# A 3x3 convolution by transformed rows: a fourth row of six with four products for its columns, the last product group added onto a preset bank, and the rows' transform back one row later

## The chip, the core and the metric

The kernel runs on one core of a Trainium2 chip. The metric is the device time of one execution in microseconds. A core has a matrix engine (TensorE, PE in the profile), a vector engine (VectorE, DVE), a scalar engine (ScalarE, ACT), GpSimd (POOL) and SyncE (SP), which issues DMAs. Each engine runs its own instructions in order and waits for others by semaphores. TensorE's results land in PSUM[...].

## The reference

Two layers on an image batch of 4 x 1024 x 56 x 56, all in 32-bit floats. Layer 0 is a bottleneck with a deformable 3x3 convolution; layer 1 is a bottleneck with batch normalisation over the whole batch. The change concerns layer 1's 3x3 convolution, 256 channels to 256, and the preparation of its filters.

```python
# layer 0
r = relu(conv1x1(x, w1, b1))                      # 1024 -> 256
r = relu(deform_conv3x3(r, w2, b2, w_off, b_off)) # offsets by a 3x3 conv, bilinear gather
x = relu(x + conv1x1(r, w3, b3))                  # 256 -> 1024
# layer 1
out = relu(bn(conv(x, w1, b1, 1, 0), g1, be1))    # 1024 -> 256
out = relu(bn(conv(out, w2, b2, 1, 1), g2, be2))  # 3x3, 256 -> 256
out = bn(conv(out, w3, b3, 1, 0), g3, be3)        # 256 -> 1024
return relu(x + softplus(residual_scale)[0] * out)
```

## The kernel before

Layer 0 fills the span to about 2060 us, with layer 1's first 1x1 convolution fused to its end; that one's output y1 goes to DRAM. Near the end of layer 0, while the last image is worked on, a generator `filters` (L651 to 706) prepares layer 1's 3x3 filters in small steps on VectorE. A step is taken by `next(extra, None)` at three of the nine taps of a block (L794).

The 3x3 convolution works on parts: half an image each, eight parts, `parts = [(n, half) ...]`. Rows go through a transform that makes six transformed rows p out of each six input rows (for four output rows, a quad; there are seven quads in a part, so a row p of a part is 128 partitions x 2 channel blocks x 7 x width). Each transformed row needs a one-dimensional convolution of three taps along its columns, with that row's own transformed filter `u[p]` (three taps u0, u1, u2 of 256 x 256). The rows are taken in the order `SEQ = (1, 2, 3, 4, 0, 5)`. Columns are kept as even and odd ones.

A row whose columns are convolved with five products (not in WIN) makes, for an even and an odd output column, products of 196 columns (and one of 203) for each of 2 x 2 blocks of channels: 20 products per row and part. A row in WIN is convolved with four products, 16 per row and part, from sums of taps (`us[p]`) and sums and differences of columns (`vs[p]`, and `v[p]` changed in place). Before, WIN is (2, 4, 5), so a part has 3 x 20 + 3 x 16 = 108 products.

A row p of part i goes through three stages on TensorE, and the loop at L1124 to 1145 interleaves them: the `begin` of a row, then the `end` of the row before it, then the row's own `middle`.

- `begin` (L993): for WIN, us x vs into bank q, then ScalarE writes the odd output columns as -2 q (L998). Otherwise two products into q and one into b; ScalarE copies q to odd (L1011) and -b to even (L1012), and VectorE adds b onto odd (L1015).
- `middle` (L1018), WIN alone: u1 x vs is added onto q, and ScalarE copies q to even (L1022).
- `end` (L1024): for WIN, u2 x v is added onto q, and u0 x v goes into a bank b; VectorE adds q onto odd (L1033) and subtracts b from even (L1034). Otherwise two more products are added onto q, and VectorE subtracts q from even (L1041). Then `end` also does the rows' transform back (L1042 to 1069): after p = 2 a sum and a difference (2 operations), after p = 4 eight operations, after p = 0 and p = 5 one each. The first and the last part also take statistics there (`bn_stats`).

ScalarE may write to the output rows of the next row only once the transform back has read them, since outputs y2 are worked on in place: `TARGET = (0, 0, 1, 2, 3, 3)` names the output row that row p uses as its place, so rows 0 and 1 share one, and rows 4 and 5.

After `end` of rows 2, 4, 0 and 5 the loop computes the next part's `inputs` for the rows that are done (L910 to 952): row transforms, then for WIN rows the column sums, L947 and its neighbour (392 elements each) and an in-place difference (L950, 784), otherwise one operation of 406 elements (L952). `load` (L876) brings the next part's input rows by DMA, and ScalarE normalises them with four activations (L901). `passes` (L1087) lets ScalarE take a middle part's statistics as sums in eight activations (L1095), two after each row, into a small tile `moved`. `reference` and `gather` (L1082, L1104) bring these sums together.

The filter taps of row 0 are written to DRAM (`u0_d`, L688) and read back at the start of the convolution (L854), as the memory is needed in between; those of row 5 are read from the input (L856). `us` of rows 2 and 4 (EARLY) are made in `filters`; those of 1, 3, 0 and 5 in the loop at L1115 to 1123, between the inputs of the first part. `first_rows` (L709) is where the first part's rows are read to, by SyncE, during layer 0.

Of the kernel before, what the change touches and what calls it, by code (L numbers as in the profile page):

```python
# [8 lines left out]
F32 = mybir.dt.float32  # L9
# [19 lines left out]
PIECE = QUADS * W  # L29
SEQ = (1, 2, 3, 4, 0, 5)  # L30
TARGET = (0, 0, 1, 2, 3, 3)
WIN = (2, 4, 5)
EARLY = (2, 4)

SIZES = (512, 512, 512, 512, 384, 384, 320)
STARTS = [sum(SIZES[:j]) for j in range(NJ)]
# [24 lines left out]
def deform_bottleneck_then_bn_bottleneck(  # L61
# [23 lines left out]

    x1_d = dram.tile([N, CIN, HW], F32, tag="x1_d", name="x1_d")
    x1_v = x1_d.rearrange("n (k p) q -> n p k q", p=128)
    u0_d = dram.tile([128, KB * 3 * CB], F32, tag="u0_d", name="u0_d")
    y1_d = dram.tile([N, CB, HW], F32, tag="y1_d", name="y1_d")
    y1_v = y1_d.rearrange("n (k p) q -> n p k q", p=128)  # L90

# [77 lines left out]
    with ExitStack() as l0:  # L169
# [481 lines left out]
        def filters():  # L651


            pool = l1.enter_context(tc.tile_pool(name="filters", bufs=1, side="right"))
            many = KB * (HALF + 2) * W
            ends = pool.tile([128, many], F32, tag="rows", name="ends")
            each = KB * 3 * CB
            w_0, w_2 = ends[:, :each], ends[:, each : 2 * each]
            for p in range(1, 5):
                u[p] = pool.tile([128, KB, 3, CB], F32, tag=f"u{p}", name=f"u{p}")  # L660
            u1, u2, u3, u4 = (u[p].rearrange("p h j o -> p (h j o)") for p in range(1, 5))
            rows = b_w2.rearrange("(h p) (i j) o -> i p h j o", p=128, j=3)
# [24 lines left out]
            nc.vector.tensor_scalar_mul(w_0, w_0, 0.25)  # L687
            nc.sync.dma_start(u0_d, w_0)  # L688
            yield
            flat = pool.tile([128, many], F32, tag="rows", name="rows")  # L690
            first_rows.append(flat.rearrange("p (h r w) -> p h r w", h=KB, w=W))
            raw_rows(first_rows[0][:, :, : HALF + 1], 0, 0)
            yield
            for p in EARLY:
                us[p] = pool.tile([128, KB, CB], F32, tag=f"us{p}", name=f"us{p}")
                yield from column_filters(p)

        def column_filters(p):

            w_0, w_1, w_2 = (u[p][:, :, j] for j in range(3))  # L700
            nc.vector.tensor_add(us[p], w_0, w_2)
            yield
            nc.vector.tensor_add(w_1, w_1, us[p])
            nc.vector.tensor_scalar_mul(w_1, w_1, 0.5)
            yield
            nc.vector.tensor_sub(us[p], us[p], w_1)
            yield

        def raw_rows(to, n, half):  # L709
# [70 lines left out]
        for i, (n, j, k) in enumerate(taps):  # L780
# [10 lines left out]
            if (n, j, k) == (N - 1, 1, 0):  # L791
                l0a.close()
                extra = filters()
            if extra and k in (1, 4, 7):  # L794
                next(extra, None)
            budget += share * SIZES[j]
            passed = (STARTS[j] + SIZES[j] * k / TAPS) / HW
# [38 lines left out]
    with l1:  # L836
# [9 lines left out]
        for p in range(6):  # L846
# [10 lines left out]
        for p in range(6):  # L857
            if p not in us:
                us[p] = wino.tile([128, KB, CB], F32, tag=f"us{p}", name=f"us{p}")
# [98 lines left out]

        half_w = W // 2

        def rows_of(n, half, r):
# [14 lines left out]
        def products(ps, terms, first=False, last=False, alone=False):  # L978

            for o in range(KB):  # L980
                of = slice(o * 128, (o + 1) * 128)
                pairs = [(wt[:, h, of], x[:, :, h]) for h in range(KB) for wt, x in terms]
                for j, (wt, x) in enumerate(pairs):
                    nc.tensor.matmul(  # L984
                        ps[:, o].rearrange("p r c -> p (r c)"),
                        wt,
                        x,
                        start=first and j == 0 and (alone or o == 0),
                        stop=last and j == len(pairs) - 1,
                        skip_group_check=not alone,  # L990
                    )

        def begin(i, p):  # L993
            even, odd = halves(i, p)
# [9 lines left out]
                first=True,  # L1004
            )
            b = bank(psb, "b", i, p, half_w + 1)
            products(b, [(u[p][:, :, 1], x0)], first=True, last=True, alone=True)
# [7 lines left out]
            nc.vector.tensor_add(odd, odd, b[..., 1:])  # L1015
            return q

        def middle(i, p, q):  # L1018
            if p in WIN:
                even, _ = halves(i, p)  # L1020
                products(q, [(u[p][:, :, 1], vs[p][..., :half_w])])
                nc.scalar.copy(even, q)  # L1022

        def end(i, p, q):  # L1024

            n, half = parts[i]
            even, odd = halves(i, p)
            if p in WIN:
                x0, x1 = v[p][..., :half_w], v[p][..., PW // 2 : PW // 2 + half_w]
                products(q, [(u[p][:, :, 2], x1)], last=True)  # L1030
                b = bank(psb, "b", i, p, half_w)
                products(b, [(u[p][:, :, 0], x0)], first=True, last=True, alone=True)
                nc.vector.tensor_add(odd, odd, q)  # L1033
                nc.vector.tensor_sub(even, even, b)  # L1034
            else:
                products(
                    q,
                    [(us[p], vs[p][..., :half_w]), (u[p][:, :, 2], vs[p][..., 1 : 1 + half_w])],
                    last=True,
                )  # L1040
                nc.vector.tensor_sub(even, even, q)  # L1041
            r = [rows_of(n, half, k) for k in range(4)]  # L1042

            def stats(k):
# [70 lines left out]
        ds = {0: load(0)}  # L1115
        for ps in ((1, 2), (3, 4), (0,), (5,)):
            inputs(0, ds[0], ps)
            for p in ps:
                if p not in WIN:
                    nc.vector.tensor_add(us[p], u[p][:, :, 0], u[p][:, :, 1])  # L1120
                elif p not in EARLY:
                    for _ in column_filters(p):
                        pass
        before, passing = None, iter(())  # L1124
        for i, p in [(i, p) for i in range(len(parts)) for p in SEQ] + [(len(parts), None)]:
            begun = begin(i, p) if p is not None else None
            if before is not None:
                j, q, _ = before
                end(*before)
                if j + 1 < len(parts) and q in (2, 4, 0, 5):  # L1130
                    inputs(j + 1, ds[j + 1], (q - 1, q) if q in (2, 4) else (q,))
                if q == SEQ[-1]:
                    if j == 0:
                        reference()
                    elif j not in ENDS:
# [9 lines left out]
            before = (i, p, begun)  # L1145
# [243 lines left out]
```

## Time and profile before

| | us |
|---|---|
| median of 3 runs | 2878.97 |
| lowest and highest | 2876.26, 2881.56 |
| the profiled execution, its own time | 2866.03 |
| its span on the core | 2864.2 |
| the 3x3 convolution of layer 1 in it | about 2097 to 2411 |
| idle time of PE at the start of that convolution (to 2105.23) | 8.43 |

TensorE's granted clock was 0.99 of full speed over the span. A 32-bit product is listed as two records, and records overlap: their listed length (329 to 339 ns at 196 columns) is longer than the distance from one to the next. In the lines of groups, the columns are: line, engine, operation, output and inputs, shape and count; then busy time and the mean of one in ns; then idle time just before, with what ended it. In the timeline: start, length, engine, line, operation, count, and in brackets the idle time before it. In the lines of waits: the engine with its line, what it waited for, the total, how many times, the longest.

### The profile page before, as it was taken

Reading aid. Unit: us, or ns where it says so; the run is one execution under the profiler, and the core shown is the slowest. Engines: PE = TensorE matmul, PEld = TensorE weight load, DVE = VectorE, ACT = ScalarE, POOL = GpSimd, SP = SyncE. Lnnn points to the kernel's source line nnn. Section 1 sums busy time; section 2 is a strip of 40 time slices with the busy share of each in tenths; the row PEclk is TensorE's granted clock in tenths of the full one; section 3 lists DMA queues with packets and bytes.
Section 4 is the critical chain, followed back from the end, with each engine's and each line's share of the span. In section 5 each row is a group of like instructions: output and inputs, shape, how many; then the busy total and the mean of one; then the engine's idle time right before and its main releaser. Section 6 shows DMA issues by size and latency. Waiting matters only on the chain.

```text
span 2864.2 us, 39301 instructions
## 1 busy us (share of the span) xinstructions
PE 2775.4 (97%) x12001; PEld 1924.8 (67%) x12001; DVE 2070.1 (72%) x4961; ACT 1503.3 (52%) x3069; POOL 1120.8 (39%) x998
## 2 busy tenths in 40 slices
PE   9978999999999999999999989999989998999999
PEld 4445566677666666667666657667779998955554
DVE  2187788888787789787888897877679886344444
ACT  2145555665556556556555656666644454244444
POOL 0065555466566556556555575544400000000000
PEclk9999999999999999999999999999999998999999
DMA  7699998999989989999998999999621102059997
GB/s 249 190 358 317 325 344 316 340 336 327 379 293 374 348 289 346 329 340 350 341 351 268 372 322 350 346 336 334 220 100 48 47 23 80 1 192 309 308 303 262
DMA packets 337109, 792.17 MB, mean 277 GB/s; under 512 B 33240, under 2 KB 183296, under 8 KB 336896
## 3 DMA queue, kind: packets, MB, share of 16 engines
q0 software_dynamic: 127296, 462.48, 45.0%
q1 hardware_dynamic: 179120, 275.78, 28.8%
q10 hardware_dynamic: 30480, 51.39, 4.7%
q8 instruction: 95, 1.56, 0.2%
q14 instruction: 118, 0.97, 0.1%
HBM read 640.68 MB, written 143.48 MB: 274 GB/s over the span
## 4 chain that ended last, share of the span: by engine, by line
PE 84%; DMA 7%; DVE 5%; ACT 2%; issue 2%; SPq 0%; POOL 0%; ACTq 0%; DVEq 0%; POOLq 0%
PE acc L540 19%; PE pf L1157 11%; PE pr L596 11%; PE acc L622 11%; PE acc L312 10%; PE q L984 7%; PE stp L512 6%; DMA g<-table,idxs 5%; DVE s L487 3%; PE acc_g L1207 2%; PE b L984 2%; PE pm L361 2%; PE ftp L391 1%; PE tp L1188 1%; PE pa L1157 1%
## 5 line engine op out<-in xcount | busy, mean ns | idle before, releaser
L475 POOL DMA_INDIRECT g<-table,idxs x900 | 1110.3, 1234 | 939.5 <-DVE s L487 283.5
L487 DVE SCALAR_TENSOR_TENSOR s<-g,wts,s 128x256 f32<-128x256 f32 (+1 forms) x2700 | 1173.3, 476 | 310.6 <-ACT s L485 299.9
L540 PE MATMUL acc<-sts,w 128*128 128x256 f32 (+2 forms) x3528 | 723.5, 355 | 5.3 <-ACT sts L518 4.1
L540 PEld LDWEIGHTS acc<-sts,w 128*128 128x128 f32 x3528 | 601.2, 190 | 56.3 <-ACT sts L518 7.4
L485 ACT ACTIVATE s<-g,wts 128x256 f32<-128x256 f32 x900 | 427.0, 511 | 285.7 <-DMA g<-table,idxs 149.4
L596 PE MATMUL pr<-r,w 128*128 128x512 f32 (+2 forms) x896 | 367.7, 548 | 19.6 <-ACT pr L592 12.8
L312 PE MATMUL acc<-xt,w 128*128 128x448 f32 x896 | 356.7, 544 | 10.7 <-DMA xt<-in_x_dram 10.7
L622 PE MATMUL acc<-x1t,c1w 128*128 128x512 f32 (+2 forms) x896 | 359.0, 542 | 6.0 <-ACT acc L618 3.8
L1157 PE MATMUL pf<-y,c3w 128*128 128x448 f32 x844 | 317.4, 539 | 0.0
L512 PEld LDWEIGHTS stp<-ident,s 128*128 128x128 f32 (+1 forms) x1800 | 212.7, 142 | 137.6 <-issue 83.4
L596 PEld LDWEIGHTS pr<-r,w 128*128 128x128 f32 x896 | 165.0, 192 | 160.6 <-issue 84.3
L1321 DVE SCALAR_TENSOR_TENSOR x1f<-pf,sc_bn,x1f 128x448 f32<-128x448 f32 x211 | 144.2, 683 | 172.5 <-PE pf L1157 159.3
L312 PEld LDWEIGHTS acc<-xt,w 128*128 128x128 f32 x896 | 168.6, 192 | 148.8 <-issue 140.6
L512 PE MATMUL stp<-ident,s 128*128 128x128 f32 (+1 forms) x1800 | 252.2, 274 | 16.6 <-DVE s L487 11.5
L1157 PEld LDWEIGHTS pf<-y,c3w 128*128 128x128 f32 x844 | 160.4, 190 | 156.8 <-issue 118.4
L622 PEld LDWEIGHTS acc<-x1t,c1w 128*128 128x128 f32 x896 | 168.0, 191 | 144.9 <-issue 90.5
L518 ACT COPY sts<-stp 128x512 f32<-128x512 f32 (+2 forms) x504 | 242.0, 529 | 13.1 <-PE stp L512 12.8
L1329 ACT ACTIVATE x1f<-x1f,sh_bn 128x448 f32<-128x448 f32 x224 | 148.3, 667 | 173.7 <-DVE x1f L1321 172.0
L607 ACT ACTIVATE x1t<-pr,ch 128x512 f32<-128x512 f32 (+2 forms) x224 | 141.6, 632 | 124.3 <-PE pr L596 121.9
L632 ACT COPY y<-acc 128x512 f32<-128x512 f32 (+2 forms) x112 | 59.3, 529 | 195.7 <-PE acc L622 195.7
L522 DVE TENSOR_TENSOR sts<-sts 128x512 f32<-128x512 f32 (+2 forms) x252 | 155.1, 615 | 0.6
L592 ACT COPY pr<-xr 128x512 f32<-128x512 f32 (+2 forms) x224 | 121.4, 542 | 4.7 <-DMA xr<-in_x_dram 0.4
(221 smaller groups left out, 2391.3 us busy)
## 6 DMA issues: line engine op xcount, KB each, us to landing
xt<-in_x_dram SPq DMA_DIRECT2D x112, 448.0 KB
x1f<-x_d SPq DMA_DIRECT2D x112, 448.0 KB
out_dram<-x1f ACTq DMA_DIRECT2D x111, 448.0 KB
xr<-in_x_dram SPq DMA_DIRECT2D x128, 256.0 KB
x_d<-x1t SPq DMA_DIRECT2D x128, 256.0 KB
table<-ft SPq DMA_DIRECT2D x56, 384.0 KB
g<-table,idxs POOLq DMA_INDIRECT x900, 7.3
xr<-in_x_dram SPq DMA_DIRECT2D x64, 192.0 KB
```

Source lines behind the costliest of these rows:

```text
L312: nc.tensor.matmul(acc, w1[:, k, h * 128 : (h + 1) * 128], xts[n, j, k - k % 2][:, k % 2, :], start=start, stop=(k == KC - 1), skip_group_ ...
L475: nc.gpsimd.indirect_dma_start(out=g[:m], out_offset=None, in_=tables[n].rearrange("r q c -> r (q c)"), in_offset=bass.IndirectOffsetOnAxi ...
L485: nc.scalar.activation(s[:m], g[:m, 0:CB], AF.Copy, scale=wt[:, 0])
L487: nc.vector.scalar_tensor_tensor(s[:m], g[:m, corner * CB : (corner + 1) * CB], wt[:, corner], s[:m], ALU.mult, ALU.add,)
L512: nc.tensor.transpose(banks[h][:, t * 128 : t * 128 + m], s[:m, h * 128 : (h + 1) * 128], ident[:m, :m],)
L518: nc.scalar.copy(to, banks[h][:, :size].rearrange("p (e q) -> p e q", e=2))
L522: nc.vector.tensor_sub(sts[:, 5:7, :half], sts[:, 1:4:2, :half], sts[:, 0:2, :half])
L540: nc.tensor.matmul(sums[i], w2[:, a, k], sts[:, b, :half], start=(k == 0 and i % 2 == 0), stop=(k == TAPS - 1), skip_group_check=True,)
L596: nc.tensor.matmul(z, w3[:, h, k * 128 : (k + 1) * 128], r2[:, h, :size], start=False, stop=(h == KB - 1), skip_group_check=True,)
L622: nc.tensor.matmul(z, c1w[:, k, h * 128 : (h + 1) * 128], x1ts[k], start=False, stop=(i == KC // 2 - 1), skip_group_check=True,)
L984: nc.tensor.matmul(ps[:, o].rearrange("p r c -> p (r c)"), wt, x, start=first and j == 0 and (alone or o == 0), stop=last and j == len(pai ...
L1157: nc.tensor.matmul(pz, c3w[:, h, k * 128 : (k + 1) * 128], y2[n][:, h, j * BLK : (j + 1) * BLK], start=(h == 0), stop=(h == KB - 1),)
```

## The change

Row 3 joins WIN and EARLY: its columns are convolved with four products as well, and its `us` is made in the early filters. Those steps are now taken at every odd tap (four of nine). Both outer rows' taps (0 and 5), with their `us` sums made in the early filters, are written to DRAM and read back, in place of row 0's taps alone; the buffer of the sums carries the tag "us2", which us[2] uses after them. At the convolution's start one addition is left (us of row 1).

In the convolution itself, from row 0 of the first part on (`on_top`), ScalarE puts -q into a bank b after a WIN row's middle, the four products u0 x v of the row's end are added onto it without a start flag, and ScalarE writes -b to the even columns, in place of VectorE's subtraction. The products into b before that no longer start for each block of output channels, but once for the bank.

The rows' transform back becomes a function of its own, `back`, and is done one row later, ahead of the begin of the row after next; `reference`, the passes' start and `gather` move along. `moved` is put into the tile of y1's statistics.

```diff
-WIN = (2, 4, 5)
-EARLY = (2, 4)
+WIN = (2, 3, 4, 5)
+EARLY = (2, 3, 4)
...
-    u0_d = dram.tile([128, KB * 3 * CB], F32, tag="u0_d", name="u0_d")
+    outer_d = dram.tile([2, 128, KB * 4 * CB], F32, tag="outer_d", name="outer_d")
...
             nc.vector.tensor_scalar_mul(w_0, w_0, 0.25)
-            nc.sync.dma_start(u0_d, w_0)
             yield
+            for i, w in enumerate((w_0, w_2)):
+                other = pool.tile([128, KB, CB], F32, tag="us2", name=f"other_{i}")
+                w = w.rearrange("p (h j o) -> p h j o", h=KB, j=3)
+                if i == 0:
+                    nc.vector.tensor_add(other, w[:, :, 0], w[:, :, 1])
+                else:
+                    yield from column_filters(w, other)
+                to = outer_d[i].rearrange("p (j o) -> p j o", j=4 * KB)
+                nc.sync.dma_start(to[:, : 3 * KB], w.rearrange("p h j o -> p (h j) o"))
+                nc.sync.dma_start(to[:, 3 * KB :], other)
...
-            if extra and k in (1, 4, 7):
+            if extra and k % 2:
                 next(extra, None)
...
-        u[0] = wino.tile([128, KB, 3, CB], F32, tag="u0", name="u0")
-        nc.sync.dma_start(u[0], u0_d.rearrange("p (h j o) -> p h j o", h=KB, j=3))
-        u[5] = wino.tile([128, KB, 3, CB], F32, tag="u5", name="u5")
-        nc.sync.dma_start(u[5], b_w2.rearrange("(h p) (i j) o -> i p h j o", p=128, j=3)[2])
...
+        for p, i in ((0, 0), (5, 1)):
+            u[p] = wino.tile([128, KB, 3, CB], F32, tag=f"u{p}", name=f"u{p}")
+            us[p] = wino.tile([128, KB, CB], F32, tag=f"us{p}", name=f"us{p}")
+            of = outer_d[i].rearrange("p (j o) -> p j o", j=4 * KB)
+            nc.sync.dma_start(u[p].rearrange("p h j o -> p (h j) o"), of[:, : 3 * KB])
+            nc.sync.dma_start(us[p], of[:, 3 * KB :])
+        us[1] = wino.tile([128, KB, CB], F32, tag="us1", name="us1")
+        nc.vector.tensor_add(us[1], u[1][:, :, 0], u[1][:, :, 1])
...
-                        start=first and j == 0 and (alone or o == 0),
+                        start=first and j == 0 and o == 0,
...
+        def on_top(i, p):
+            return (i, SEQ.index(p)) >= (0, 4)
...
         def middle(i, p, q):
             if p in WIN:
                 even, _ = halves(i, p)
                 products(q, [(u[p][:, :, 1], vs[p][..., :half_w])])
-                nc.scalar.copy(even, q)
+                if on_top(i, p):
+                    ends[i, p] = bank(psb, "b", i, p, half_w)
+                    nc.scalar.mul(ends[i, p], q, -1.0)
+                else:
+                    nc.scalar.copy(even, q)
...
-                b = bank(psb, "b", i, p, half_w)
-                products(b, [(u[p][:, :, 0], x0)], first=True, last=True, alone=True)
+                b = ends.pop((i, p), None)
+                top = b is not None
+                if not top:
+                    b = bank(psb, "b", i, p, half_w)
+                products(b, [(u[p][:, :, 0], x0)], first=not top, last=True)
                 nc.vector.tensor_add(odd, odd, q)
-                nc.vector.tensor_sub(even, even, b)
+                if top:
+                    nc.scalar.mul(even, b, -1.0)
+                else:
+                    nc.vector.tensor_sub(even, even, b)
...
-        moved = wino.tile([128, 2, KB, between * CUTS], F32, tag="moved", name="moved")
+        moved = y1_stats.rearrange("p h s -> p (h s)")[:, : 2 * KB * between * CUTS].rearrange(
+            "p (f h c) -> p f h c", f=2, h=KB
+        )
...
-        before, passing = None, iter(())
-        for i, p in [(i, p) for i in range(len(parts)) for p in SEQ] + [(len(parts), None)]:
+        before, behind, passing = None, None, iter(())
+        for i, p in [(i, p) for i in range(len(parts)) for p in SEQ] + [(len(parts), None)] * 2:
+            if behind is not None:
+                back(*behind)
+                if behind[1] == SEQ[-1]:
+                    if behind[0] == 0:
+                        reference()
+                    elif behind[0] not in ENDS:
+                        passing = passes(behind[0])
+                if behind == (len(parts) - 1, SEQ[-2]):
+                    gather()
             begun = begin(i, p) if p is not None else None
+            behind = None
             if before is not None:
                 j, q, _ = before
                 end(*before)
+                behind = j, q
                 if j + 1 < len(parts) and q in (2, 4, 0, 5):
                     inputs(j + 1, ds[j + 1], (q - 1, q) if q in (2, 4) else (q,))
-                if q == SEQ[-1]:
-                    if j == 0:
-                        reference()
-                    elif j not in ENDS:
-                        passing = passes(j)
-                for _ in range(2):
-                    next(passing, None)
-                if (j, q) == (len(parts) - 1, SEQ[-2]):
-                    gather()
+            for _ in range(2):
+                next(passing, None)
```

More of the change, by code (lines that the diff above doesn't have):

```diff
@@ L695, in filters, with column_filters @@
                 us[p] = pool.tile([128, KB, CB], F32, tag=f"us{p}", name=f"us{p}")
[L696 to L701, printed above, removed]
+                yield from column_filters(u[p], us[p])
+        def column_filters(w, other):
+            w_0, w_1, w_2 = (w[:, :, j] for j in range(3))
+            nc.vector.tensor_add(other, w_0, w_2)
             yield
-            nc.vector.tensor_add(w_1, w_1, us[p])
+            nc.vector.tensor_add(w_1, w_1, other)
             nc.vector.tensor_scalar_mul(w_1, w_1, 0.5)
-            yield
-            nc.vector.tensor_sub(us[p], us[p], w_1)
+            nc.vector.tensor_sub(other, other, w_1)
             yield
@@ L852, in deform_bottleneck_then_bn_bottleneck @@
             vs.append(wino.tile([128, QUADS, KB, width], F32, tag=f"vs{p}", name=f"vs{p}"))
-        u[0] = wino.tile([128, KB, 3, CB], F32, tag="u0", name="u0")
-        nc.sync.dma_start(u[0], u0_d.rearrange("p (h j o) -> p h j o", h=KB, j=3))
-        u[5] = wino.tile([128, KB, 3, CB], F32, tag="u5", name="u5")
-        nc.sync.dma_start(u[5], b_w2.rearrange("(h p) (i j) o -> i p h j o", p=128, j=3)[2])
-        for p in range(6):
-            if p not in us:
-                us[p] = wino.tile([128, KB, CB], F32, tag=f"us{p}", name=f"us{p}")
+        for p, i in ((0, 0), (5, 1)):
[6 more added lines that the diff above has]
+        nc.vector.tensor_add(us[1], u[1][:, :, 0], u[1][:, :, 1])
         sum_t = wino.tile([128, KB, QUADS, W], F32, tag="sum_t", name="sum_t")
@@ L976, in bank, with products @@
             return t[:, : KB * QUADS * width].rearrange("p (o r c) -> p o r c", o=KB, c=width)
-        def products(ps, terms, first=False, last=False, alone=False):
+        def products(ps, terms, first=False, last=False):
             for o in range(KB):
@@ L987, in products @@
                         x,
-                        start=first and j == 0 and (alone or o == 0),
+                        start=first and j == 0 and o == 0,
                         stop=last and j == len(pairs) - 1,
-                        skip_group_check=not alone,
+                        skip_group_check=True,
                     )
+        def on_top(i, p):
+            return (i, SEQ.index(p)) >= (0, 4)
         def begin(i, p):
@@ L1006, in begin @@
             b = bank(psb, "b", i, p, half_w + 1)
-            products(b, [(u[p][:, :, 1], x0)], first=True, last=True, alone=True)
+            products(b, [(u[p][:, :, 1], x0)], first=True, last=True)
             for o in [slice(o, o + 1) for o in range(KB)] if p == 1 else [slice(0, KB)]:
@@ L1016, in begin @@
             return q
+        ends = {}
         def middle(i, p, q):
@@ L1021, in middle @@
                 products(q, [(u[p][:, :, 1], vs[p][..., :half_w])])
-                nc.scalar.copy(even, q)
+                if on_top(i, p):
[3 more added lines that the diff above has]
+                    nc.scalar.copy(even, q)
         def end(i, p, q):
-            n, half = parts[i]
             even, odd = halves(i, p)
@@ L1041, in end, with back @@
                 nc.vector.tensor_sub(even, even, q)
+        def back(i, p):
+            n, half = parts[i]
             r = [rows_of(n, half, k) for k in range(4)]
@@ L1117, in deform_bottleneck_then_bn_bottleneck @@
             inputs(0, ds[0], ps)
[L1118 to L1123, printed above, removed]
-        before, passing = None, iter(())
-        for i, p in [(i, p) for i in range(len(parts)) for p in SEQ] + [(len(parts), None)]:
+        before, behind, passing = None, None, iter(())
[9 more added lines that the diff above has]
+                    gather()
             begun = begin(i, p) if p is not None else None
+            behind = None
             if before is not None:
@@ L1144, in deform_bottleneck_then_bn_bottleneck @@
                 ds[i + 1] = load(i + 1)
-            before = (i, p, begun)
+            before = (i, p, begun) if p is not None else None
     sc2, sh2 = scale_shift(y2_stats, KB, cols("g2", KB), cols("be2", KB), "bn2")
```

## The prediction

> **What bounds the kernel now.** I read the page's sums and its chain first, then stretches of one part each (a part is half an image, eight parts in all) through the 3x3 convolution of the second layer at 2097 to 2411 us, then the waits, and last the order of instructions at the places where an engine stands.
>
> ```profile
> PE 2775.4 (97%) x12001; PEld 1924.8 (67%) x12001; DVE 2070.1 (72%) x4961; ACT 1503.3 (52%) x3069; POOL 1120.8 (39%) x998
> PE 84%; DMA 7%; DVE 5%; ACT 2%; issue 2%; SPq 0%; POOL 0%; ACTq 0%; DVEq 0%; POOLq 0%
> ...
> 2143.00:2180.00 37.00, 37.00 (x220) 36.76 (x219) 36.92 (x61) 11.11 (x19) 0.56 (x4) 1.00 0.14 45
> 2180.00:2217.00 37.00, 36.98 (x219) 36.41 (x218) 34.88 (x52) 19.29 (x39) 0.75 (x5) 1.00 0.15 48
> 2217.00:2254.00 37.00, 36.85 (x214) 35.59 (x213) 32.11 (x49) 19.26 (x38) 0.37 (x3) 1.00 0.15 46
> ```
>
> The first two lines say that TensorE carries the end. The last three are stretches of 37 us (start:end, length, PE, PEld, DVE, ACT, POOL, clock, DMA share, GB/s): TensorE is full in all of them, but VectorE is too in the second part (36.92 of 37) and has only 5 us to spare later, while ScalarE has 18. So work taken off TensorE pays only where VectorE keeps up. TensorE's busy time is flattered by overlapping records. The first product of consecutive parts starts (L1011's releaser) 37.15 us apart on average, and 108 products of 0.337 us (two records of 0.168) make 36.4, so 0.75 us per part is standing time. The waits show whom it stands for:
>
> ```profile
> PEld q L984 <- ACT y L1022: 3.7, 12, 0.6
> PEld q L984 <- ACT y L998: 1.7, 6, 0.4
> ```
>
> A four-product row ("WIN") hands its bank q to ScalarE twice and then adds to it. TensorE needs other products to fill that time. Without them the gap looks like the stage's end:
>
> ```profile
> 2400.14 1.50 PE L984 MATMUL b<-v,u 128*128 128x196 f32 x8
> 2404.35 2.98 PE L984 MATMUL q<-vs,u 128*128 128x196 f32 x8 [2.71 <-ACT y L998]
> 2407.93 2.98 PE L984 MATMUL q<-v,u 128*128 128x196 f32 x8 [0.59 <-ACT y L1022]
> ```
>
> From the end of a group to the next on the same bank takes 0.6 to 0.76 us ([...]ScalarE's 0.52, signals), and eight records after the pause cost 2.98 instead of 1.36.
>
> **The skill.** "TensorE: Matmul & The Clock Gate", Part 1: after an idle window the array runs at half rate until it has been busy a window long. The trace agrees on the half rate (2.98 against 1.36), though a pause of 2.71 us sufficed here. "PSUM — Partial Sum Buffer", the four PSUM rules: writes of ScalarE leave the accumulate bits as they are, and a matmul without start adds where a bit is set. So the preset bank can work; layer 0 of this kernel shows the same pattern (L592 into pr, then L596). "Perfetto Trace Analysis", on the most contended engine: weight-load time tells more than matmul busy; here it does (35.59 of 37 where PE reads 36.85).
>
> **The change, part by part.**
>
> *Row 3 with four products.* Per part 20 products (16 of 196 columns, 4 of 203) become 16: 4 x 0.336 plus the 203-column surcharge of 4 x 0.008 is 1.38 us. Eight parts: **-11.1**.
>
> *VectorE per part.* Row 3's inputs gain two operations of 392 elements and an in-place one of 784 and lose one of 406. By start-to-start pace (0.475, 0.885, 0.49): 2 x 0.475 + 0.885 - 0.49 = +1.35.
>
> ```profile
> L950 DVE TENSOR_TENSOR v<-v 128x784 f32<-128x784 f32 x21 | 20.3, 965 | 0.5
> L952 DVE SCALAR_TENSOR_TENSOR vs<-v 128x406 f32<-128x406 f32 x21 | 12.0, 572 | 0.0
> L1034 DVE TENSOR_TENSOR y<-y,b 128x392 f32<-128x392 f32 x24 | 13.4, 559 | 5.5 <-ACT y L1022 2.9 <-PE b L984 2.3
> L1022 ACT COPY y<-q 128x392 f32<-128x392 f32 x24 | 12.4, 518 | 33.8 <-PE q L984 33.7
> ```
>
> The ends lose the subtraction of L1034 in rows 2, 4 and 5 and row 3's end goes from two operations to one: -4 x 0.475 = -1.9. Net -0.55 per part from part 1 on; VectorE drops to about 31.6 of a 35.8 us part. ScalarE takes four writes of 0.52 more, +2.1 per part, for 21 of 36. Neither is the bound by its sum, but ScalarE's order now matters: its write stands between two product groups.
>
> *Stage start.* Before, VectorE adds us for rows 1 and 3 (1.29 us together) ahead of the first inputs; after, only row 1's: TensorE starts 0.6 us earlier, **-0.6**. Off VectorE's list in the head also go us0's addition (0.6) and u5's four filter operations (2.2). But row 3's extra halves (about 2) and part 1's inputs of rows 3 and 4 (4.5) now all stand ahead of the transform back of row 4, because that comes a row later. Row 5's first product is read (L998) only once that transform has written its target: at 2146.28 before, by my list at about 2149 after. Row 5's middle waits, and its cover is spent: **+2.8**, and +0.5 in part 1, where VectorE is still full. Bounds: nothing, if VectorE gains on its list, to +4.5.
>
> *New waits between groups.* Row 3's begin is followed by the end of row 2 and then row 3's middle. Where row 2's end was held, q3's begin and middle meet, and the round trip of 0.76 is open. I find that in parts 2, 3, 4, 5, 7: **+3.8** (0 to 5.3). ScalarE's new preset is queued, in order, behind the statistics passes and the four rows of the next part:
>
> ```profile
> 2227.34 0.83 ACT passed L1095
> 2228.17 0.03 issue
> 2228.20 0.19 ACT passed L1095
> 2228.39 1.05 ACT rows L901
> 2229.43 0.93 ACT passed L1095 x2
> 2230.36 3.04 ACT rows L901 x3
> 2233.40 0.93 ACT passed L1095 x2
> 2234.34 0.40 ACT y L1022
> ```
>
> This is before's chain of waits: about 7 us of ScalarE ahead of a copy that TensorE needs. In part 2 row 3's end comes out 1.1 us late behind it (**+1.1**). In part 6 row 2's middle waits for L998's successor, queued behind passes and rows, while TensorE has only the last rows of part 5 to fill: 3.1 to 3.5, taken 3.3, and as such a pause is longer than 2.7 us, half-rate records after it (0 to 2, taken 1.5): **+4.8**. The other parts come out hidden. Against that, some of before's 0.75 per part (6.0 in all) goes, since row 3's groups now give cover elsewhere: between 0 and 6, taken **-2.0**.
>
> *Row back one later.* It keeps the six to eight operations of row 4's transform from standing between a row's end and the next inputs. No operation is added; its price is the +2.8 above.
>
> *Tail.* Before, b's products of row 5 filled the gap at 2400.14. On top, they come last, after ScalarE's preset: 4 products, 1.35 at full and 3.0 at half rate; by the lines above TensorE is at half rate there, but the round trip of the preset runs beside q's end, so **+2.2**. ScalarE's negation (0.52) replaces VectorE's (0.56): nothing.
>
> *Filters in layer 0.* About nine VectorE operations, 5.0 us, join the filter steps at 1640 to 1740, and SyncE writes 2 MB instead of 0.77.
>
> ```profile
> 1680.00:1700.00 20.00, 16.16 (x70) 11.32 (x68) 17.89 (x43) 11.25 (x24) 15.97 (x10) 1.00 0.88 294
> ...
> 1720.00:1740.00 20.00, 20.00 (x91) 14.73 (x90) 14.76 (x36) 13.93 (x30) 8.95 (x10) 1.00 1.02 388
> ```
>
> The added steps fall after 1700, where TensorE is full and VectorE has 5 of 20 us free; so they cost nothing while that cover lasts, and up to 5 without it. The second outer row's sum uses the same buffer as the first's and waits for that write (SyncE's u0_d write took 3.3 to 3.7 us): 0 to 2 on VectorE. The first rows' read (2 x 0.8 MB) moves behind these writes, away from 1699, where a gather stood 5.09 us and TensorE 3.88; that could give back 3, and DMA at 1.02 of its share at 1720 could take 3. Taken **0**, range -3 to +3. The remaining edits (the sums of the passes in the tile of the first statistics, outer rows read in place of added up) hide under DMA time at the layer's turn.
>
> **Sum.** -11.1 - 0.6 + 2.8 + 0.5 + 3.8 + 1.1 + 4.8 - 2.0 + 2.2 + 0 = +1.5 against the profiled run's 2866.03 (span 2864.2). Runs have a median of 2878.97, 12.9 above; I carry the difference over unchanged: 2880.5.
>
> **Rivals.**
> *B, the products' gain arrives.* For it: VectorE and ScalarE both have slack by sums, and three of my waits rest on an order that a shift of 1 us dissolves. Only the head (+3.3), two round trips (+1.5) and the tail (+2.2) stay, and 3 of the old pauses go: -11.1 - 0.6 + 3.3 + 1.5 + 2.2 - 3.0 = -7.7, 2871.3. Against: the waits on L1022 and L998 already exist at lower stakes.
> *C, ScalarE's queue becomes TensorE's gate (slower).* Place: the preset and q's copies behind passes and rows in parts 2 to 6. Price: the mean of 1.1 and 3.3 in each of five parts, 11.0, round trips in seven parts 5.3, half rate 1.5: -11.1 - 0.6 + 3.3 + 5.3 + 11.0 + 1.5 + 2.2 - 2.0 = +9.6, 2888.6. It decides from the point where TensorE's waits on ScalarE within the stage, half rate included, exceed before's by 14.0 us: 8.2 make good what the other terms save (11.1 + 0.6 + 2.0 - 3.3 - 2.2), and 5.8 more can be seen. A has 9.7 of them, C 17.8. For it: 7 us of ScalarE in one block. Against: ScalarE idles 18 of 37.
> *D, the change does less than it says:* on-top rows begin only with row 0 of part 0, so 29 of 32 rows have them; four-product row 3 is unconditional. That the stage shows no fewer products: 2879.
>
> **How the numbers follow.** A (+1.5, own range 2875 to 2886) 0.48, B 0.23, C 0.27, D 0.02. What a measurement can tell from no change is 0.2%, 5.8 us. Faster by more: most of B and little of A, 0.23. Slower by more: C and the upper edge of A, 0.30. Within: 0.47. The range, 2870 to 2891, takes in the centres of B and C and leaves out the far halves of their tails, with layer 0's 3 us at either side.
>
> **What would show it.** Right: the stage has 832 instead of 864 products; L984's wait on ScalarE's first read of row 3's bank about 0.7 us in several parts; row 5's read in part 0 near 2149; one pause over 2.5 us in part 6; b's last products after 2405, at half rate. Wrong: part periods near 35.8 us (then B), waits on ScalarE in parts 2 to 6 of 2 us and more each (then C), or the stage beginning more than 3 us off 2097 (then layer 0 decides, and my zero for the filters fails).

## The result, and the profile after

The changed kernel takes 2889.51 us (median of 22 runs) against 2877.87 for the kernel before (22 runs): a ratio of 1.0036, 95% interval 1.0024 to 1.0047, so about 10 us slower. Its profiled execution has a span of 2889.8 us. That is 25.6 more than the profiled execution of before, but layer 0 differs from one execution to the next: at gather number 675 (counted from 0), ahead of anything that the change touches, the changed kernel is already 9.9 us late, and by number 765 it has lost another 4.9. I therefore compare the 3x3 stage by itself, from the start of its first product to the end of its last (lines q and b of TensorE). It is 305.7 us before and 316.6 after: **+10.9**, which accounts for the whole of the measured difference.

Where it went, from mark to mark, with the forecast's terms of the same stretch. A part's mark is the start of ScalarE's first read of its row 1 (L1026; L1011 before):

| stretch | before | after | change | forecast |
|---|---|---|---|---|
| first product to part 0's mark | 6.32 | 8.44 | +2.1 | -0.6 |
| part 0 | 31.72 | 30.43 | -1.3 | -1.4 |
| part 1 | 36.61 | 40.13 | +3.5 | +1.9 |
| part 2 | 36.93 | 37.43 | +0.5 | +0.5 |
| parts 3, 4, 5 | 112.09 | 110.17 | -1.9 | -1.9 |
| part 6 | 37.25 | 43.70 | +6.4 | +3.4 |
| part 7 and the tail | 44.75 | 46.29 | +1.5 | +1.6 |
| old pauses that go | | | | -2.0 |

The page's line of engines, of the changed kernel:

```profile
PE 2779.4 (96%) x11937; PEld 1924.6 (67%) x11937; DVE 2068.6 (72%) x4953; ACT 1515.0 (52%) x3098; POOL 1120.9 (39%) x1005
```

The products are gone: 11937 records listed instead of 12001, 64 fewer (32 products of two records). TensorE's waits within the stage, of the changed kernel (what waited, for what, total, times, longest):

```profile
PE q L996 <- ACT y L1013: 14.1, 12, 4.0
PE q L996 <- DVE v L946: 8.7, 2, 8.3
PE q L996 <- DVE y L1067: 3.1, 1, 3.1
PE q L996 <- ACT b L1041: 1.9, 2, 1.3
```

Of L946's 8.7 us, 8.3 lie ahead of the stage's first product. The visible pauses within the stage have grown from 3.8 us to 19.4. Most of this, 14.1, is for L1013, ScalarE's first read of a WIN row's bank (the PSUM tile, 512 floats per partition, in which its products are added up), and only 1.9 for the new preset L1041. Three long pauses make 9.5 of the 14.1: 2.78, 2.71 and 4.04. The windows of parts 1, 2, 3 and 6 (columns as before) show where:

```profile
2158.70:2198.83 40.13, 37.34 (x210) 36.46 (x209) 38.21 (x62) 12.65 (x22) 0.68 (x5) 0.96 0.13 41
2198.83:2236.26 37.43, 35.51 (x210) 34.91 (x209) 31.09 (x45) 20.80 (x42) 0.88 (x6) 1.00 0.15 47
2236.26:2273.36 37.10, 36.04 (x210) 34.85 (x209) 31.79 (x49) 20.05 (x39) 0.49 (x4) 1.00 0.14 44
2346.44:2390.14 43.70, 37.52 (x210) 36.28 (x209) 32.53 (x48) 21.00 (x43) 0.69 (x5) 0.96 0.06 19
```

The two long parts are the ones with a clock of 0.96. The pause that starts it in part 1 is in the chain of waits (start, length, piece):

```profile
2165.24 0.97 DVE y L1091 x2
2166.20 0.02 issue
2166.22 0.53 ACT y L1013
2166.75 0.04 issue
2166.80 3.50 PE q L996 x10
```

ScalarE may write row 5's odd columns only when the last operation of row 4's transform back, L1091, has read them, since rows 4 and 5 use the same output row and the transform keeps its difference r2 - r3 in it. Before, this point was 2146.28, or 3.0 us after the part's mark; now it is 2166.22, or 7.5 us after it. TensorE's timeline in part 6 shows the same wait, and a second one after it:

```profile
2354.76 2.98 PE L996 MATMUL q<-vs,u 128*128 128x196 f32 x8 [2.71 <-ACT y L1013]
2357.53 1.66 PE L996 MATMUL b<-v,u 128*128 128x203 f32 x8
...
2366.28 2.97 PE L996 MATMUL q<-v,u 128*128 128x196 f32 x16 [3.06 <-DVE y L1067]
```

ScalarE's and VectorE's timelines there, a line of each:

```profile
2354.17 0.53 ACT L1013 ACTIVATE y<-q 128x392 f32<-128x392 f32 x1 [6.98 <-DVE y L1091]
```

```profile
2360.02 0.56 DVE L1030 TENSOR_TENSOR y<-y,b 128x392 f32<-128x392 f32 x1 [3.67 <-ACT y L1027]
```

ScalarE had nothing to do for 6.98 us before it could read the bank. The first pause holds row 1's products into b back, so VectorE idles 3.67 us in front of L1030, and does its queue (inputs, row 5's transform back, then the subtraction L1067 that frees row 1's bank) later. TensorE needs that bank and pauses a second time. At the tail TensorE's pause is 4.04 instead of 2.71, and b's products follow at half rate:

```profile
2427.30 2.98 PE L996 MATMUL q<-vs,u 128*128 128x196 f32 x8 [4.04 <-ACT y L1013]
2430.86 2.98 PE L996 MATMUL q<-v,u 128*128 128x196 f32 x8 [0.57 <-ACT b L1041]
2433.63 2.79 PE L996 MATMUL b<-v,u 128*128 128x196 f32 x8
```

### The profile page after: what moved, and what is told of

Read it like the earlier page. It is cut to its first block, busy times and chain, and to the rows that moved or that the text cites. A ratio compares the mean times of both kernels' runs of the same rounds, so it can differ in the third digit from the quotient of the medians.

```text
span 2889.8 us, 39264 instructions
## 1 busy us (share of the span) xinstructions
PE 2779.4 (96%) x11937; PEld 1924.6 (67%) x11937; DVE 2068.6 (72%) x4953; ACT 1515.0 (52%) x3098; POOL 1120.9 (39%) x1005
## 4 chain that ended last, share of the span: by engine, by line
PE 81%; DVE 7%; DMA 7%; ACT 3%; issue 2%; SPq 0%; POOLq 0%; DVEq 0%; ACTq 0%; another core or an unknown queue 0%; POOL 0%
PE acc L541 18%; PE pf L1188 11%; PE pr L597 11%; PE acc L623 10%; PE acc L313 10%; PE stp L513 6%; PE q L996 6%; DMA g<-table,idxs 5%; DVE s L488 3%; PE acc_g L1238 2%; PE pm L362 2%; PE b L996 2%; PE ftp L392 1%; PE tp L1219 1%; ACT rows L911 1%
## 5 line engine op out<-in xcount | busy, mean ns | idle before, releaser
L519 ACT COPY sts<-stp 128x512 f32<-128x512 f32 (+2 forms) x504 | 242.2, 529 | 21.8 <-PE stp L513 14.6
```

Of the source, the lines that this page charges most:

```text
L519: nc.scalar.copy(to, banks[h][:, :size].rearrange("p (e q) -> p e q", e=2))
```

## The experiments

Every one is read by its stage length, which was 305.7 and 304.8 in two profiles of the kernel before. The instructions' order within an engine is planned when the kernel is built, so an edit also moves other instructions; a stage length holds both. Ratios are to the kernel before on the same chip.

A stage length also holds chance, above all at its two ends. This is the tail of the kernel before in its second profile:

```profile
2408.49 2.98 PE L984 MATMUL q<-vs,u 128*128 128x196 f32 x8 [2.71 <-ACT y L998]
2412.07 1.63 PE L984 MATMUL q<-v,u 128*128 128x196 f32 x8 [0.59 <-ACT y L1022]
```

The pauses are those of the first profile, shown in the prediction, but there the second group took 2.98 us as well: half rate in one execution, full rate in the other. From part 7's mark to the end it is 44.75 and 43.39 us, from the first product to part 0's mark 6.32 and 6.84; between these two marks it is 254.6 in both. So where a small difference lies is said below.

**1. Nothing on top.** `on_top` returns False.

```diff
-            return (i, SEQ.index(p)) >= (0, 4)
+            return False
```

> No row goes on top: a WIN row's last four products start their own bank again and VectorE subtracts it; row 3 keeps four products and the transform back stays a row late. Measure: the length of the 3x3 stage from its first product to its last (305.7 us before, 316.6 after). Theory 1 (row 5's middle waits for row 4's late transform back, and b's four products, no longer free to run in that wait, were its cover): the pauses before row 5's middle in parts 1 and 6 shrink from 2.8 and 2.7 to about 1.4 and the tail gives 2.5 back: stage 307 to 311, total -6 to -9 against the changed kernel. Rival (ScalarE's extra writes as such are the gate): the same or more, 305 or less. Rival (row 3's round trips): 315 to 317, nothing gained.

Stage 293.9, ratio 0.9956 (0.9942 to 0.997): 12.7 us faster than before by the medians. So the on-top rows alone turn a gain of 11.8 us into a loss of 10.9: 22.7 us. That is far more than my theory gave them. By size the rival (ScalarE's extra writes) fits better here; experiments 4 and 6 decide between the two. One pause of 2.73 is left, in the tail, with two groups of eight records at full rate behind it (1.59 and 1.63 us):

```profile
2386.53 1.59 PE L996 MATMUL q<-vs,u 128*128 128x196 f32 x8 [2.73 <-ACT y L1013]
```

The kernel before had half rate behind such a pause, so up to about 3 of the 22.7 us may be chance (my estimate: 2.98 less 1.6, twice).

**2. The transform back at once.** `back(*behind)` and what follows it move from ahead of `begin` to right behind `end`.

> The rows' transform back stands right behind the row's end again, all else as in the changed kernel. Theory 1: row 4's transform is done about 2 to 3 us sooner in parts 0 and 5, so the pauses of 2.8 and 2.7 before row 5's middle go, with the half rate after them: stage 309 to 312; the tail's pause of 4.0 stays. Rival (ScalarE's extra writes): no change, 316 to 317. Rival (VectorE is full, so that whatever it does first makes the other late): 315 to 320, with the wait moved to the inputs of the next part.

Stage 302.8, ratio 0.9987 (0.9977 to 0.9996). Parts 1 and 6 fall from 40.1 and 43.7 to 35.1 and 39.4, the tail keeps its pause of 4.01. With all of ScalarE's extra writes in place, 13.8 us go: the writes by themselves aren't the gate. Part 6 keeps pauses of 0.87 (L1013 on L1091), 1.74 (on VectorE's L1067) and 0.98 (on L1013, behind ScalarE's passes and rows).

**3. Row 3 with five products.**

```diff
-WIN = (2, 3, 4, 5)
-EARLY = (2, 3, 4)
+WIN = (2, 4, 5)
+EARLY = (2, 4)
```

> Row 3 has five products again (its inputs and sums as before), with on-top rows, the filters' outer rows and the late transform back as in the changed kernel. Theory 1 (row 3's saving of 11.1 us is real and the other parts of the change eat it): stage 321 to 328. Rival (row 3 brings the loss itself, by VectorE's added 1.35 us of inputs and by its round trips): 308 to 316.

With this, row 3's `us` is added at the stage's start again. Stage 312.3, ratio 1.0027 (1.0016 to 1.0039). Taking the fourth row away makes the changed kernel 4.3 us shorter, so in this setting row 3's saving is not only eaten, it makes the waits worse. The rival's range is met, not mine; that it isn't row 3 by itself, experiment 8 shows.

**4. Row 5 not on top.** `return i > 0 and p != 5`.

> Rows 2, 3 and 4 go on top from part 1 on, row 5 never. Theory 1 (only row 5's four products of b were cover in a long wait): nearly all that the kernel without any on-top row gains, stage 307 to 311. Rival (ScalarE's queue, all on-top rows alike): a quarter of it, 314 to 316.

Stage 300.7, ratio 0.998 (0.997 to 0.999). Row 5 alone accounts for 15.9 of the 22.7 us of experiment 1, although it is 8 of 29 on-top rows (one in four). Its products into b ran inside the wait for row 4's transform before (at the tail, the 1.50 us at 2400.14 in the prediction); on top they come after it.

**5. Nothing on top, transform back at once.** Experiments 1 and 2 together.

> No row on top, and the transform back right behind the row's end: of the changed convolution only row 3's four products are left. Stage lengths so far: 305.7 before, 316.6 changed, 293.9 without on-top rows, 302.8 with on-top rows and the transform back at once. Theory (the late transform hurts only where b's products are no cover): 292 to 296, level with 293.9. Rival (the late transform is worth something of its own, taking eight operations from between a row's end and the next inputs): 297 to 300. Rival (it hurts in any case): 291 or less.

Stage 297.5, ratio 0.9975 (0.995 to 1.0001). By its whole length the late transform by itself is worth 3.6 us (297.5 to 293.9), as the rival had it. But all of this lies behind part 7's mark (44.41 against 40.58): a pause of 3.71 instead of 2.73, and two groups of 2.98 instead of 1.59 and 1.63. Up to that mark the two are level (253.1 and 253.4), as the theory had it, so a worth of the late transform outside the tail isn't shown, and 2.7 of the 3.6 are TensorE's rate there. With on-top rows it costs 13.8. The two edits harm each other; on-top rows with the transform at once cost 5.3.

**6. A tile of its own for the difference.** Row 4's transform leaves its difference r2 - r3 in `dif_t` and no longer in row 3 of the output; `passed`, which nobody reads, is kept in 16 bits to make room.

```diff
-                nc.vector.tensor_sub(r[3], r[2], r[3])
+                nc.vector.tensor_sub(dif_t, r[2], r[3])
```

> On-top rows and late transform as in the changed kernel, but the transform back of row 4 puts its difference into a tile of its own, no longer into the output row that row 5 is written to (the passes' unread output is kept in 16 bits to make room). Row 5's first read by ScalarE then waits for the transform's second operation, not its eighth. Theory (the wait runs through that output row): the pauses before row 5's middle in parts 1 and 6 fall below 0.8 us, the tail's of 4.0 below 1.0, stage 298 to 305. Rival (ScalarE's preset and negation in order are the gate by themselves): 312 to 317.

Stage 290.3, ratio 0.9949 (0.9929 to 0.9968). All of the change is in it, and 26.3 us of stage go. TensorE's waits for ScalarE in that run's stage:

```profile
PE q L997 <- ACT b L1042: 0.6, 1, 0.6
PE q L997 <- ACT y L1014: 0.3, 1, 0.3
```

The line of 14.1 us is down to 0.3 (L1014 is L1013 here), with ScalarE as loaded as in the changed kernel: 115.8 us from part 1's mark to part 7's against 115.4, and a pass takes 948 ns with the 16-bit output and 947 without. (By the code, row 4's transform is nine operations, two, two, one and four, where eight are named further up; the last four read the difference.) The tail has no pause before row 5's middle, and the last groups run at the full rate:

```profile
2396.59 1.82 PE L997 MATMUL q<-vs,u 128*128 128x196 f32 x10
2398.98 1.63 PE L997 MATMUL q<-v,u 128*128 128x196 f32 x8 [0.57 <-ACT b L1042]
```

What remains of the preset is its 0.57 at the end. That ScalarE's preset and negation are the gate by themselves is ruled out.

**7. The same tile, nothing on top.**

> The same tile for the difference, without on-top rows. Theory: the last pause of 2.7 us at the end and the half-rate records behind it (2 x 1.6) go: stage 288 to 291. If that pause has another cause: 293 to 295.

Stage 285.8, ratio 0.9937 (0.9913 to 0.996), the fastest of all; its interval overlaps those of 1 and 6. 832 products of 0.337 us are 280.4. The tail's pause is gone:

```profile
2402.16 1.82 PE L997 MATMUL q<-vs,u 128*128 128x196 f32 x10
```

Half-rate records had no part in the gain, since experiment 1's tail had none: the tail gives 3.7 of the 8.1 us, the way to part 0's mark 1.7, the parts between the rest. Even without the wait, on-top rows cost 4.5 us by the whole length (290.3 to 285.8). But 1.7 of these lie ahead of part 0's mark (8.44 against 6.73), before the first on-top row, where only TensorE's rate differs; 2.8 are left.

**8. Row 3 with five products, nothing on top.** Experiments 1 and 3 together.

> Row 3 with five products and no on-top rows, transform back late, filters as in the changed kernel: against 293.9 it prices row 3 by itself. Theory (row 3's 32 products of 0.34 us come through whole when nothing is on top): 303 to 306. Rival (row 3 pays only in part, since VectorE's longer inputs and its round trips take some back): 297 to 301.

Stage 302.3 against 293.9 of experiment 1: row 3's four products are worth 8.4 us of the 11.1 counted, between the two ranges. From part 0's mark on it is 11.2 (296.7 to 285.5), the whole of the count; ahead of the mark 2.8 are lost (5.60 to 8.44), 1.0 of it because VectorE's inputs come later, most of the rest at a lower rate. The run's ratio, 1.0016 (1.0 to 1.0031), is about 8 us above what its stage says (3.4 below before). I can't explain that; its profiled layer 0 was the longest of all, and experiment 3, with the same edit ahead of the stage, shows no such excess.

**9. The filters' part alone.** Experiments 3 and 5 together: outer rows and sums written and read back, steps at odd taps.

> Of the change only the filters' part is left: both outer rows and their sums written and read back, steps at every odd tap, one or two additions at the stage's start; three rows of four products, nothing on top, transform back at once. Theory (the filters' part hides under layer 0's TensorE): stage 305 to 306.5, total within 3 us of before (ratio 0.999 to 1.001). Rival (its VectorE steps and the 2 MB it writes cost layer 0 time): ratio 1.001 to 1.003, with the gathers from the 675th to the 765th taking 2 to 5 us longer than in the same chip's profile of the kernel before.

Ratio 1.0004 (0.9989 to 1.0019), stage 303.6: a little under the range, 1.2 to 2.0 us shorter than before. None of this lies between the marks of parts 0 and 7 (254.7 against 254.6), so it is no sign of a gain. The stretch from gather 675 to gather 765 took 205.7 us here, against 194.3 in before's profile, but see the next.

**10. The kernel before again.**

> The kernel before, once more: a second profile of it on the chip of the other runs, to show how far layer 0 moves from one execution to the next. Ratio 1.000; stage 305.7 within 0.5; if the time from the 675th to the 765th gather lies at 197 or above here (194.3 in the first profile), the filters' part isn't what lengthens it.

Ratio 0.9996 (0.9982 to 1.001), stage 304.8: 0.9 under the first profile where 0.5 was expected, by the rate in the tail. That stretch took 200.0 us, 5.7 more than in the first profile of the same program, and in experiment 1, with the changed filters, 192.2. So the changed kernel's 199.2 is no sign of the filters' price. Their price is within what experiment 9's interval allows, -3.2 to +5.5 us; a small one can't be told from none.

**11. Row 4's transform back at once, the others late.**

```diff
-                back(*behind)
+                if behind[1] != 4:
+                    back(*behind)
...
                 behind = j, q
+                if q == 4:
+                    back(j, q)
```

> On-top rows and late transform as in the changed kernel, except that row 4's transform back stands right behind row 4's end. Theory (of the late transform only row 4's, whose output row 5 needs, does harm): stage 298 to 304, as with every transform at once (302.8) or below. Rival (the harm is in the other rows' transforms, which delay VectorE's last subtraction of row 1 and so a bank): 312 to 317.

Stage 302.8, the same as with all of them at once, ratio 0.9982 (0.9969 to 0.9995). The harm of the late transform is row 4's.

**12. The kernel before with the difference in its own tile.**

> The kernel before, with nothing of the change, but with the transform back's difference in a tile of its own. Theory (the wait of row 5 through that output row was there before, hidden but for the tail, where it costs a pause of 2.7 us and two groups at half rate): the tail's pause goes and little else, stage 299 to 302, ratio 0.997 to 0.9995. Rival (it is the late transform alone that makes the wait matter): 304 to 306.

Stage 296.5, ratio 0.9982 (0.9966 to 0.9997). That is 8 to 9 us less, below the range; by the ratio about 5 (1 to 10). The theory had the place right: 7 to 8 of them lie behind part 7's mark (36.58 against 44.75 and 43.39), where both pauses and all half-rate groups are gone, and 0.4 between the marks of parts 0 and 7 (254.2 against 254.6). So the wait was there before the change, and what it cost it cost at the tail. This gain needs nothing of the change.

The stage lengths side by side (row 3 with four products):

| | on top | nothing on top |
|---|---|---|
| transform late, difference in the output row | 316.6 (the change) | 293.9 |
| transform at once, difference in the output row | 302.8 | 297.5 |
| transform late, difference in its own tile | 290.3 | 285.8 |

## Why the prediction was right or wrong

The time fell into the range, at its slower end. What had been held likeliest, less than 5.8 us either way (0.47), did not come; slower by more had 0.30. The likeliest case (+1.5) was too good by 9. Rival C had the size (+9.6), and its first sign came too: TensorE's pauses for ScalarE grew from 3.6 to 16.0 us, with half rate by about 16 (my estimate, from groups of 2.98 us against 1.6), more than the 14.0 asked for. But 9.5 of these pass through ScalarE only, whose read was itself waiting for VectorE's transform. C's other sign, 2 us and more in each of parts 2 to 6, came in part 6 alone (1.9 in part 2, about 1.0 in 3 to 5). So the size of C was luck, and its mechanism was not what cost most.

- **Products, -11.1.** The count came as said (64 records); 8 x 1.38 is 11.0. Experiments 1 and 8 give 8.4 us of it, 11.2 from part 0's mark on, and 7 against 12 gives 10.7 together with the late transform and the filters: right, once nothing waits.
- **Stage start, -0.6.** Wrong. TensorE started 339.60 us after the 765th gather, before 339.76: 0.2 of 0.6. And part 0's mark came 2.1 us later, as VectorE's inputs for the second channel block reached TensorE 0.96 us later and the next 12 records took 4.29 us at a low rate instead of 3.12. I had counted only the additions taken off the list and not the order of the rest. The rate isn't bound to that order: experiment 7 has the same 0.96 and reaches the mark after 6.73 us instead of 8.44.
- **Row 4's transform late, +3.3.** Place and cause right (L1013 on L1091; forecast 2.7 us later than the 3.0 after the mark, measured 7.5 after it, so 4.5 later). The pause was 2.78, as forecast; missing were the eight records after it at half rate (2.98 instead of 1.36). I had priced the half rate in part 6 and at the tail only. Part 1 lost 4.9 beyond its share of products, not 3.3.
- **Round trips, +3.8, and part 2, +1.1.** Right. In parts 2, 3, 4, 5 and 7 TensorE pauses 0.61 or 0.62 us between a row's first and second group (row 3's, by the order of the groups), 3.1 in all, and in part 2 it waits 1.29 for the preset L1041. Parts 2 to 5 came out within 0.1 us of the forecast together.
- **Part 6, +4.8.** The stretch was right, row and reason of the long pause were not, and this is the step that failed; that the stretch was right is in part luck. I put the pause before row 2's middle, on ScalarE's queue behind passes and rows; it came before the middle of part 5's row 5. The trace shows ScalarE idle for 6.98 us in front of L1013 and VectorE's L1091 as its releaser; experiment 2 takes 4.3 us of the part away and experiment 6 brings it to 35.9 with ScalarE's queue unchanged in load. I also missed the second pause, 3.06, VectorE held in front of L1030 by the first: +7.8 beyond the products. The queue that I had named is there behind both: the next L1013 stands behind four row activations (2365.11 to 2369.18), but TensorE's visible pause for it is 0.38, and 0.98 in experiment 2.
- **Old pauses, -2.0.** No stretch shows this gain; parts 2 to 5 come out as forecast without it. It couldn't come from visible pauses: those of the kernel before, between its first product and the tail, are 0.7 us in all.
- **Tail, +2.2.** With part 7's round trip +3.0 forecast, +2.9 measured. "TensorE is at half rate there" was right: 2.79 us for eight records.
- **Filters, 0.** Ratio 1.0004 by themselves. The sign that this zero fails did come, as the stage began 14.6 us later than before; but 9.9 of it arose ahead of the filters' first step, and the other 4.9 is less than the 5.7 by which experiment 10 differs from the first profile.

The four misses (2.7 at the start, 1.6 in part 1, 3.0 in part 6, 2.0 of old pauses) make 9.3 of the 9.4 us between +1.5 and +10.9. Common to the second and third: each long pause was taken at its own length, while in this profile it also brought half rate, and in part 6 a second wait.

What I had written of VectorE's and ScalarE's loads held (31 to 32.5 and 20 to 21 us in parts 2, 3 and 6), and was no use as an argument: in the changed kernel both have slack (VectorE 5 to 11 us, but for part 1), and TensorE still waits. Rival B would have come true without on-top rows: experiment 1 gives -11.8 in the stage.

Not tried: on-top rows with the order of each engine held fixed, which would separate the preset's own price from that of the new order.

## What to carry to other kernels

Before a product group is made to depend on another engine's write, look whether it is what fills TensorE's time in a wait next to it; row 5's four products were 15.9 of 22.7 us. When an operation is postponed, look which place it reads that someone else waits to overwrite: a difference kept in the output row held the next row back through nine operations, and a tile of its own gave 26 us in the changed kernel, where reordering gave 14, and 8 to 9 in the kernel before. Two edits that share one wait have to be tried together and apart. Before a difference of 2 or 3 us is put down to an edit, look in which stretch it lies: some here lay where the edit had not begun to act.

## What the runs showed of the hardware

A pause's length alone did not decide on the half rate. After pauses of 2.71 and 2.78 us in the changed kernel the next eight records took 2.98 us; after 2.73 in experiment 1 they took 1.59, and after 3.06 in part 6, 16 records took 2.97, the full rate, as after 3.07 in experiment 3. Not even the program decided: after the same two pauses, 2.71 and 0.59, the second group of the kernel before took 2.98 in one profile and 1.63 in the other. The Trainium skill ("TensorE: Matmul & The Clock Gate", Part 1) says that the gate watches a free-running window of about 3.4 us. A window that starts anywhere would fit this, but no run here shows the window itself, and pauses shorter than that sufficed. At the tail of the changed kernel a pause of 4.04 us and one of 0.57 kept 24 records at 2.8 to 3.0 us per eight.

Two profiles of one program differ by 5.7 us in the same 90 gathers of layer 0, as much as 0.2% of the whole time.
